# A Perceiver-style block with routed experts on one core: rests of 33 to 96 tokens as three groups, branches ahead of the last tile, context tails on 128 rows

## The chip, the cores and the metric

The kernel runs on one core of one Trainium2 chip. The metric is the device time of one execution in microseconds, the median of three runs. The names of the engines are those of the profile: PE multiplies matrices (PEld is its weight load), DVE and ACT do elementwise work, POOL issues the indirect transfers, SP issues the loads. A word on PE's records: a float32 matmul of this kernel shows as two records, a transpose as one.

## The reference, cut to what matters

All values are float32; there are 8 sequences of 64 tokens, 512 tokens of width 512.

```python
# 1. cross-attention to a context of 1601 rows per sequence
p = layernorm(x)                                   # 8 x 64 x 512
q = ctx @ W.T + b
x = x + relu(softmax(p @ q.T) @ ctx @ W.T + b)
# 2. causal linear attention with 16 heads of 64, then a gelu MLP of width 2048
h = layernorm(x)
h = h + attention(ln(h)) @ wo
h = h + gelu(ln(h) @ w1 + b1) @ w2 + b2
x = x + h
# 3. experts: 8 experts of width 1024, each token goes to its best two
m = layernorm(x); logits = m @ w_router
for e in range(8):
    out += gating[:, e] * ((silu(m @ w0[e]) * (m @ w1[e])) @ wo[e])
x = x + out
```

The number of tokens that each expert receives is data. For the inputs given, the reference's router sends 133, 104, 217, 159, 87, 132, 70 and 122 tokens to experts 0 to 7 (worked out by evaluating the reference up to its router).

## The kernel before, in words

The order of the instructions on every engine is the order in which the program writes them; no scheduler moves them.

**Cross-attention.** Tokens are taken in four tiles `t` of two sequences. `key_group(t, g)` multiplies the tile with one of four pieces of the transposed context (`ctxT`), `softmax(t)` and `turn_scores(t)` make the transposed weights `eT`, and `weigh(t, g)` multiplies them with the context rows (`ctx`), three pieces of 512 rows and then a tail. 1601 = 3 x 512 + 65, so the tail is 65 rows: it is loaded to 65 partitions (`tail`, L188), its weights are turned by one transpose (L464), and it closes the sum with two matmuls over 65 rows (L487). DVE then scales the sum by the reciprocal of the row sums (`av_sb`, L495). The context comes in through SP's queue into a ring of 12 buffers, in an order written out by hand. At the end of tile `t = 1`, `late_loads` (L408 to L412) puts five small transfers on the same queue: zeros to the spare rows of the output, zeros to a table, a bias, and `proj` twice; `centre_router` (L548) is four small matmuls.

**Experts.** The router's ranks are written to a table in DRAM; from it POOL gathers each expert's first 128 tokens (key `(e, 0)`) and the next few, 32 of them (key `(e, 1)`). `whole_tile` takes 128 tokens through one expert: four quarters `up` (L1200), silu and product, transposes `ht`, `down` (L1208); `between(k)` slips the transposes `xgt` of later tokens in between. `add_rows` scales the result on ACT (`y_sb`, L1180) and POOL adds it to the output with an indirect transfer (L1181). After each tile stands a branch, `tc.If(few_of[e] > 0)` (L1429): where the expert has 129 to 160 tokens, `group` takes the rest, up to 32 tokens, through the same weights, the four quarters side by side in four column strips of PE's array (L1238, L1249), and sums the strips with one more matmul, `fold` (L1259). Experts with more than 160 tokens are listed, and each further set of 128 tokens becomes a "big" tile behind the last expert: `all_big` (L1433) nests seven branches, and each `big_tile` loads the six weight buffers of its expert again. For these inputs the groups behind experts 0, 3 and 5 run (5, 31 and 4 tokens) and one big tile runs, the remaining 89 tokens of expert 2.

A branch that is not taken ends in a small block of its own, in which each engine waits until its own work is done, and then raises its counters by what the skipped block would have raised them.

Of the kernel before, what the change touches and what calls it, by code (L numbers as in the profile page):

```python
# [26 lines left out]
NG = LK // GK  # L27
TAIL = LK - NG * GK
SW = -(-LK // 4)
# [5 lines left out]
FQ = FE // NQ  # L35
R = P // NQ
NI = B * S // P
COLS = 4 * KC + FF // P + KC * NE
# [8 lines left out]
def perceiver_kernel(  # L47
# [127 lines left out]
    def issue_to(n):  # L175

        while issued[0] < min(n, len(order)):
            key, src = order[issued[0]]
            if in_ring(key) and len(held) >= RING:
                if held[0] not in freed:  # L180
                    return
                held.pop(0)
            if key in places_of:
                t_ = places_of[key]
                nc.sync.dma_start(t_, src)
            elif key[0] == "tail":
                t_ = tails.tile([P, 2, D], F32, tag="tail", name="_".join(str(k) for k in key))
                nc.sync.dma_start(t_[:TAIL, :, :], src)  # L188
            else:
                width = WIDTHS[key[2]] if key[0] == "ctxT" else 512  # L190
                t_ = ring.tile([P, 4, width], F32, tag="ring", name="_".join(str(k) for k in key))
                nc.sync.dma_start(t_, src)
                held.append(key)
            streamed[key] = t_
            issued[0] += 1
# [254 lines left out]
    def turn_scores(t):  # L450
# [5 lines left out]
        for g in range(NG + 1):  # L456
            bank = mm_bank(f"et_{t}_{g}")
            if g < NG:
                for j in range(4):
                    k = g * GK + j * P  # L460
                    nc.tensor.transpose(bank[:, j * P : (j + 1) * P], scores[:, k : k + P], ident)
                nc.scalar.copy(e_t[:, 4 * g : 4 * g + 4, :].rearrange("p j q -> p (j q)"), bank)
            else:
                nc.tensor.transpose(bank[:TAIL, :P], scores[:, NG * GK : LK], ident)  # L464
                nc.scalar.copy(e_t[:TAIL, 4 * NG, :], bank[:TAIL, :P])

    all_av, all_xo = {}, {}

    def weigh(t, g):
# [15 lines left out]
        if g == NG - 1:  # L485
            for h in range(2):
                nc.tensor.matmul(  # L487
                    av[h * S : (h + 1) * S, :],
                    e_t[:TAIL, 4 * NG, h * S : (h + 1) * S],
                    need("tail", t)[:TAIL, h, :],  # L490
                    start=False,
                    stop=True,
                )
            av_sb = all_av[t] = xa2.tile([P, D], F32, tag="tmp", name=f"av_sb_{t}")
            nc.vector.tensor_scalar(av_sb, av, all_rinv[t], None, ALU.mult)  # L495

# [65 lines left out]
    for t in range(NT):  # L562
# [14 lines left out]
        weigh(t, 2)  # L577
        if t == NT - 3:
            late_loads()
            centre_router()  # L580
# [530 lines left out]
    if True:  # L1111
# [36 lines left out]
        def turn_tile(key, n=P):  # L1148
# [4 lines left out]
            for c in range(KC):  # L1153
                nc.tensor.transpose(  # L1154
                    bank[:, c * n : (c + 1) * n], xg[:n, c * P : (c + 1) * P], ident[:n, :n]
                )
            xg_t = moe2.tile([P, KC, n], F32, tag=f"xgT{n}", name=f"xgT_{key[0]}_{key[1]}")
            evacuate(xg_t.rearrange("p c q -> p (c q)"), bank[:, : KC * n])
# [71 lines left out]
        def group(e, up_of, down_of):  # L1230
# [3 lines left out]
            xg_t = turned[e, 1]  # L1234
            bank = side_bank(1, f"up_{nm}")
            for c in range(KC):
                for q in range(NQ):
                    nc.tensor.matmul(  # L1238
                        bank[q * R : (q + 1) * R, :],
                        xg_t[c],  # L1240
                        up_of[q][:, c, :],
                        start=(c == 0),
                        stop=(c == KC - 1),
                    )
            h_t = hidden_t(1, gated(1, bank, nm), nm)
            bank = side_bank(1, f"yq_{nm}")
            for j in range(2):
                for q in range(NQ):
                    nc.tensor.matmul(  # L1249
                        bank[q * R : (q + 1) * R, :],  # L1250
                        h_t[:, j, q * R : (q + 1) * R],
                        down_of[q // 2][:, 2 * (q % 2) + j, :],
                        start=(j == 0),
                        stop=(j == 1),
                    )
            parts = moe2.tile([P, D], F32, tag="parts", bufs=1, name=f"parts_{nm}")
            evacuate(parts, bank)
            y = y_bank(1, f"y_{nm}")
            nc.tensor.matmul(y[:R, :], fold, parts, start=True, stop=True)  # L1259
            add_rows((e, 1), y, R, 1)  # L1260

        if True:
# [7 lines left out]


            few = moe.tile([P, NE], F32, name="few")
            more = moe.tile([P, NE, NI - 1], F32, name="more")
            nc.vector.tensor_scalar(more[:, :, 0], count, float(P + R), None, ALU.is_gt)
            nc.vector.scalar_tensor_tensor(few, count, float(P), more[:, :, 0], ALU.is_gt, ALU.subtract)
            few_i = moe.tile([1, NE], mybir.dt.int32, name="few_i")
# [3 lines left out]
            def load_few():  # L1280
                _, values = nc.values_load_multi_w_load_instructions(
                    few_i, min_val=0, max_val=1, skip_runtime_bounds_check_because=counted
                )
# [3 lines left out]
            flat = "p e i -> p (e i)"  # L1287
            control = moe.tile([1, 1 + 2 * NBIG], mybir.dt.int32, name="control")

            def list_big(k):  # L1290

                if k == 0:
# [10 lines left out]
                    listed["sums"] = sums  # L1303
                    nc.vector.tensor_copy(control[:, 0:1], sums[0:1, nmore - 1 :])
                else:
                    by_big = [P, NBIG, nmore]
# [11 lines left out]
                    for v, values in enumerate([number, which_e]):  # L1318
# [6 lines left out]
                        )  # L1325
                    nc.vector.tensor_copy(control[:, 1:], numbers[0:1, :])
                    listed["big_e"] = numbers[:, NBIG:]

            def load_big():
# [11 lines left out]
                _, experts = nc.values_load_multi_w_load_instructions(  # L1341
                    control[:, 1 + NBIG :],
                    engines=sp,
# [3 lines left out]
                )  # L1347
                return big, spots, experts

# [11 lines left out]
            def gate_big(j):  # L1361
# [11 lines left out]
                slots["big", j] += (gate,)  # L1373

            def big_tile(j):

                key = ("big", j)
                tiles = {}
                e = bass.ds(listed["experts"][j], 1)
                for q in range(NQ):  # L1380
                    tiles["up", q] = ring.tile([P, 4, 512], F32, tag="ring", name=f"big_up_{j}_{q}")
                    nc.sync.dma_start(tiles["up", q], e_up[e, q].rearrange("o p c n -> p (o c) n"))
                    if q % 2:
                        n = q // 2
                        tiles["wo", n] = ring.tile([P, 4, 512], F32, tag="ring", name=f"big_wo_{j}_{n}")
                        nc.sync.dma_start(
                            tiles["wo", n],
                            e_wo[e, n].rearrange("o p c n -> p (o c) n"),
                        )

# [8 lines left out]
                )  # L1399

            turned[0, 0] = [xg_t0[c // 2][:, c % 2, :] for c in range(KC)]
            for e in range(NE):

                def between(k, e=e):
                    if e == 0 and k == 0:
                        late_places()
                        for key in [(1, 0), (0, 1), (0, 0), (1, 1), (2, 0), (2, 1)]:
                            fetch(key, R if key[1] else P)
                    if k == (2 if e == 0 else 1) and e + 1 < NE:
                        turn_tile((e + 1, 0))  # L1410
                    if k == 2:
                        turn_tile((e, 1), R)
                    if e == 1 and k < 2:
                        list_big(k)

                up_of = [need("e_up", e, q) for q in range(NQ)]
                down_of = [need("e_wo", e, n) for n in range(2)]
                whole_tile((e, 0), up_of, down_of, between)
                if e == 0:
                    few_of = load_few()  # L1420
                if 3 <= e + 2 < NE:
                    for i in range(2):
                        fetch((e + 2, i), R if i else P)
                if e == 3:
                    listed["big"], listed["spots"], listed["experts"] = load_big()
                    listed["pairs"] = read_big(0)
                if e == NE - 3:
                    fetch_big(0, listed["pairs"])
                with tc.If(few_of[e] > 0):  # L1429
                    group(e, up_of, down_of)  # L1430

            def all_big(j):
                with tc.If(listed["big"] > j):  # L1433
                    big_tile(j)
                    if j + 1 < NBIG:
                        all_big(j + 1)

            all_big(0)


# [90 lines left out]
```

## Time and profile before

| | us |
|---|---|
| median of 3 runs (663.93 to 664.02) | 663.94 |
| the profiled execution's own time | 665.04 |
| its span, first to last instruction | 663.3 |
| PE busy | 624.8 (94%) |
| DVE, ACT, POOL busy | 175.4, 128.9, 61.8 |
| mean granted PE clock | 0.987 |

How to read it: the span begins with the cross-attention (to about 185 us), then linear attention (to about 290 us), the MLP (to about 410 us) and the router; the first expert's tile starts at 417.26 us and the last result is written behind 652.98 us. PE is busy nearly everywhere, so time comes from the places where it isn't, from the work that it is given, and from the end.

### The profile page before, as it was taken

The numbers are of one execution on the slowest core, as the hardware profiler recorded it, in microseconds if no ns is written. First come the engines' busy times: TensorE is split into PE (matmuls) and PEld (weight loads), VectorE is DVE, ScalarE is ACT, GpSimd is POOL, SyncE is SP. The second block draws the span as 40 slices with busy tenths as digits, with TensorE's granted clock in tenths as the row PEclk, the third lists the DMA queues.
The fourth block names the chain that finished last, engine by engine and source line by source line (L and its number), as shares of the span: only waits on it lengthen the run. The fifth ranks groups of instructions, "written<-read, shape, count | busy, mean of one in ns | idle before, by whom it ended". The sixth has DMA issues, their size and how long they took to land. (4 is left out here: it accounts for less than half of the span.)

```text
span 663.3 us, 6862 instructions
## 1 busy us (share of the span) xinstructions
PE 624.8 (94%) x2688; PEld 292.5 (44%) x2688; DVE 175.4 (26%) x421; ACT 128.9 (19%) x242; POOL 61.8 (9%) x82
## 2 busy tenths in 40 slices
PE   4998999899999999999999999999999899999993
PEld 3743434243444444455444458434444344344441
DVE  4011323123315878760000045311211011100100
ACT  2241222220132222031101211211111111111110
POOL 2000000000000000050000012240201202200000
PEclk9998999899999999999999999999999999999997
DMA  8999999999430303030311313139379567594611
GB/s 325 418 424 398 423 393 422 381 394 417 178 126 3 126 1 127 1 126 1 126 64 63 116 74 133 64 96 365 139 280 377 178 279 246 202 385 155 263 16 19
DMA packets 24224, 138.08 MB, mean 208 GB/s; under 512 B 4164, under 2 KB 4164, under 8 KB 11896
## 3 DMA queue, kind: packets, MB, share of 16 engines
q1 hardware_dynamic: 20056, 129.90, 49.8%
q0 software_dynamic: 3024, 6.58, 4.4%
q10 hardware_dynamic: 1104, 1.07, 0.5%
q8 instruction: 25, 0.41, 0.3%
q14 instruction: 15, 0.12, 0.0%
HBM read 132.56 MB, written 4.97 MB: 207 GB/s over the span
## 5 line engine op out<-in xcount | busy, mean ns | idle before, releaser
L1200 PE MATMUL up<-e_up,xgT 128*128 128x512 f32 x224 | 100.2, 595 | 1.2 <-PEq L1429 1.2
L1200 PEld LDWEIGHTS up<-e_up,xgT 128*128 128x128 f32 x224 | 40.9, 190 | 50.4 <-issue 50.4
L1208 PE MATMUL y<-e_wo,hidT 128*128 128x512 f32 x128 | 61.0, 599 | 0.0
L477 PE MATMUL av<-ctx,eT 128*64 128x512 f32 x192 | 51.3, 648 | 6.3 <-DMA ctx<-in_ctx_dram 6.3
L1165 DVE TENSOR_TENSOR mid<-up,act 128x256 f32<-128x256 f32 x35 | 14.8, 425 | 159.4 <-ACT act L1163 159.4
L809 PE MATMUL hid<-v_sb,w 128*128 128x512 f32 (+2 forms) x144 | 56.6, 545 | 0.0
L830 PE MATMUL mlp<-w,hid_sb 128*128 128x512 f32 x112 | 51.0, 597 | 0.0
L428 PE MATMUL sc<-ctxT,pw_t 128*64 128x401 f32 (+1 forms) x256 | 46.6, 501 | 0.0
L809 PEld LDWEIGHTS hid<-v_sb,w 128*128 128x128 f32 x144 | 26.2, 190 | 29.1 <-issue 27.3
L1163 ACT ACTIVATE act<-up 128x256 f32<-128x256 f32 x35 | 13.3, 384 | 103.7 <-PE up L1200 94.9
L1181 POOL DMA_INDIRECT out_dram<-y_sb,dst_late x11 | 16.8, 1530 | 159.9 <-ACTq L1429 103.7
L824 POOL TENSOR_TENSOR xin<-xin,b_bc 128x512 f32<-128x512 f32 x4 | 5.1, 1265 | 283.2 <-DVE rstd_h L766 279.0
L830 PEld LDWEIGHTS mlp<-w,hid_sb 128*128 128x128 f32 x112 | 20.7, 190 | 23.5 <-issue 23.4
L1208 PEld LDWEIGHTS y<-e_wo,hidT 128*128 128x128 f32 x128 | 22.4, 190 | 19.5 <-issue 19.1
L428 PEld LDWEIGHTS sc<-ctxT,pw_t 128*64 128x64 f32 x256 | 20.6, 136 | 23.4 <-issue 21.7
L477 PEld LDWEIGHTS av<-ctx,eT 128*64 128x64 f32 x192 | 14.7, 146 | 36.1 <-issue 27.5
L728 PE MATMUL wo<-wo,a_t 128*128 128x512 f32 x64 | 29.1, 600 | 0.6 <-DVE a_t L704 0.6
L617 PE MATMUL wk<-h_t,wk 128*128 128x512 f32 x64 | 29.5, 603 | 0.0
L617 PE MATMUL wq<-h_t,wq 128*128 128x512 f32 x64 | 29.4, 602 | 0.0
L537 PE MATMUL v<-wv,h_t 128*128 128x512 f32 x64 | 28.7, 597 | 0.6 <-DVE h_t L524 0.6
L702 DVE RECIPROCAL rden<-rden 128x512 f32<-128x512 f32 x8 | 26.8, 3353 | 0.3
L878 DVE TENSOR_TENSOR xs<-mlp,xs 128x512 f32<-128x512 f32 x3 | 2.1, 692 | 86.6 <-PE mlp L830 86.6
(245 smaller groups left out, 642.6 us busy)
## 6 DMA issues: line engine op xcount, KB each, us to landing
e_up<-in_L_ffn_up_dram SPq DMA_DIRECT2D x32, 1024.0 KB, 7.7
ctx<-in_ctx_dram SPq DMA_DIRECT2D x24, 1024.0 KB, 17.1
ctxT<-in_ctx_T_dram SPq DMA_DIRECT2D x24, 802.0 KB, 15.7
e_wo<-in_L_ffn_wo_dram SPq DMA_DIRECT2D x16, 1024.0 KB, 10.6
w<-in_L_attn_w_dram SPq DMA_DIRECT2D x8, 1024.0 KB, 9.8
ctxT<-in_ctx_T_dram SPq DMA_DIRECT2D x8, 796.0 KB, 16.4
big_up<-in_L_ffn_up_dram SPq DMA_DIRECT2D x4, 1024.0 KB, 7.7
wv<-in_L_attn_wv_dram SPq DMA_DIRECT2D x2, 1024.0 KB, 13.0
```

Source lines behind the costliest of these rows:

```text
L428: nc.tensor.matmul(sc[h * S : (h + 1) * S, :width], pw_t[:, c, (2 * t + h) * S : (2 * t + h + 1) * S], keys[h][:, c, :], start=(c == 0), s ...
L477: nc.tensor.matmul(av[h * S : (h + 1) * S, :], e_t[:, 4 * g + j, h * S : (h + 1) * S], rows[h][:, j, :], start=(g == 0 and j == 0), stop=F ...
L537: nc.tensor.matmul(bank, h_t[:, c, t * P : (t + 1) * P], wv_n[:, c, :], start=(c == 0), stop=(c == KC - 1))
L617: nc.tensor.matmul(bank, w[:, c, (j % 4) * P : (j % 4 + 1) * P], h_t[:, c, :], start=(c == 0), stop=(c == KC - 1),)
L702: nc.vector.reciprocal(rden, rden)
L728: nc.tensor.matmul(wo_banks[t], a_t[:, j, t * P : (t + 1) * P], wo_r[j // 4][:, j % 4, :], start=(j == 0), stop=(j == nj - 1),)
L809: nc.tensor.matmul(hid_banks[f][:, tokens], w[:, c, (f % 4) * P : (f % 4 + 1) * P], h2_t[:, c, tokens], start=(c == 0), stop=(c == KC - 1),)
L830: nc.tensor.matmul(acc[t], hid[:, t * P : (t + 1) * P], need("w2", f // 4)[:, f % 4, :], start=(f == 0), stop=(f == FF // P - 1),)
L1165: nc.vector.tensor_tensor(hid, bank[:, FQ:], act, ALU.mult)
L1181: nc.gpsimd.indirect_dma_start(out=out, out_offset=bass.IndirectOffsetOnAxis(ap=dst[:n, :], axis=0), in_=y_sb[:n, :], in_offset=None, boun ...
L1200: nc.tensor.matmul(bank, xg_t[c], up_of[q][:, c, :], start=(c == 0), stop=(c == KC - 1))
L1208: nc.tensor.matmul(y, h_t[:, j, :], w[:, 2 * (q % 2) + j, :], start=(q + j == 0), stop=(q + j == NQ))
```

## The change

Four things are altered.

1. The tail is one row shorter, 64 rows. The two sequences' tails are stacked on 128 partitions (the host lays them out so), and beside them stands the last context row, copied to 64 partitions for each sequence. The tail's weights are turned by two 64x64 matmuls against the identity; the tail's two products use two quarters of the array; the last row is added on DVE by a multiply and add, ahead of the scaling. The tail's transfer grows from 65 to 128 rows of 4 KB.
2. `late_loads` and `centre_router` stand at the end of tile 2 instead of tile 1.
3. A rest of 33 to 96 tokens is no longer a big tile: `three_groups` takes it behind the expert's own tile, as three groups of 32. The gathers of `(e, 1)` fetch 96 rows. Each expert therefore has two branches, one for three groups and one for a group. `group` itself is written in two halves of 128 hidden columns, so that silu and product of the first half run beside the second half's matmuls, and the second product is cut into halves of 256 columns.
4. The branches of experts 6 and 7 and the big tiles stand ahead of the last expert's tile, inside one more branch on "any of them". In the middle of each tile a prefetch hint names the branch ahead as likely taken. One more control value is loaded into registers on every engine after expert 3's tile. Big tiles reuse weight buffers instead of taking new ones.

The diff, cut to its core:

```diff
-TAIL = LK - NG * GK
+TAIL = LK - NG * GK - 1
+REST = 3 * R
...
-                nc.sync.dma_start(t_[:TAIL, :, :], src)
+                nc.sync.dma_start(t_, src)
...
-                nc.tensor.transpose(bank[:TAIL, :P], scores[:, NG * GK : LK], ident)
-                nc.scalar.copy(e_t[:TAIL, 4 * NG, :], bank[:TAIL, :P])
+                for h in range(2):
+                    part = slice(h * S, (h + 1) * S)
+                    nc.tensor.matmul(
+                        bank[part, :S],
+                        scores[part, NG * GK : NG * GK + TAIL],
+                        ident[part, part],
+                        start=True,
+                        stop=True,
+                    )
+                nc.scalar.copy(e_t[:, 4 * NG, :S], bank[:, :S])
...
-                    e_t[:TAIL, 4 * NG, h * S : (h + 1) * S],
-                    need("tail", t)[:TAIL, h, :],
+                    e_t[h * S : (h + 1) * S, 4 * NG, :S],
+                    need("tail", t)[h * S : (h + 1) * S, 0, :],
...
-            nc.vector.tensor_scalar(av_sb, av, all_rinv[t], None, ALU.mult)
+            nc.vector.scalar_tensor_tensor(
+                av_sb, need("tail", t)[:, 1, :], all_scores[t][:, LK - 1 : LK], av, ALU.mult, ALU.add
+            )
+            nc.vector.tensor_scalar(av_sb, av_sb, all_rinv[t], None, ALU.mult)
...
-        if t == NT - 3:
+        if t == NT - 2:
             late_loads()
             centre_router()
...
         def group(e, up_of, down_of):
...
+            for h in range(2):
+                bank = side_bank(1, f"up_{nm}_{h}")
+                for c in range(KC):
+                    for q in range(NQ):
+                        nc.tensor.matmul(
+                            bank[q * R : (q + 1) * R, : 2 * P].rearrange(split, w=2),
+                            xg_t[c],
+                            up_of[q][:, c, :].rearrange(split, w=2)[:, :, halves[h]],
+                            start=(c == 0),
+                            stop=(c == KC - 1),
+                        )
+                act = moe2.tile([P, P], F32, tag="act1", name=f"act_{nm}_{h}")
+                nc.scalar.activation(act, bank[:, :P], AF.Silu)
+                hid.append(moe2.tile([P, P], F32, tag="mid1", name=f"mid_{nm}_{h}"))
+                nc.vector.tensor_tensor(hid[h], bank[:, P : 2 * P], act, ALU.mult)
...
+            turn(0)
+            down(0, 0)
+            turn(1)
+            down(0, 1)
+            parts = []
+            for n in range(2):
+                down(1, n)
+                parts.append(moe2.tile([P, D // 2], F32, tag="parts", name=f"parts_{nm}_{n}"))
+                (nc.scalar.copy if n else nc.vector.tensor_copy)(parts[n], sums[n][:, : D // 2])
+            y = side_bank(1, f"y_{nm}")
+            for n in range(2):
+                nc.tensor.matmul(
+                    y[:R, n * D // 2 : (n + 1) * D // 2], fold, parts[n], start=True, stop=True
+                )
             add_rows((e, 1), y, R, 1)
+
+        def three_groups(e, up_of, down_of):
+            xg = fetched[e, 1]
+            bank = y_bank(1, f"xgt3_{nm}")
+            for c in range(KC):
+                nc.tensor.transpose(
+                    bank[:, c * REST : (c + 1) * REST], xg[:REST, c * P : (c + 1) * P], ident[:REST, :REST]
+                )
...
+            up(0)
+            up(1)
+            turn(0)
+            up(2)
+            turn(1)
+            down(0)
+            down(1)
+            turn(2)
+            y = side_bank(1, f"y3_{nm}")
+            folded(0)
+            down(2)
+            folded(1)
+            folded(2)
+            add_rows((e, 1), y, REST, 1)
...
-            nc.vector.tensor_scalar(more[:, :, 0], count, float(P + R), None, ALU.is_gt)
+            nc.vector.tensor_scalar(more[:, :, 0], count, float(P + REST), None, ALU.is_gt)
...
+            def few_tokens(e, up_of, down_of):
+                with tc.If(few_of[e] == 1, label=f"three_{e}"):
+                    three_groups(e, up_of, down_of)
+                with tc.If(few_of[e] == 2):
+                    group(e, up_of, down_of)
+
+            def hint_ahead(e):
+                with tc.block():
+                    tc.mark_branch_hint_location("last_branches" if e == NE - 2 else f"three_{e}", "LikelyTaken", engines=every)
...
                 def between(k, e=e):
+                    if k == 0 and e < NE - 1:
+                        hint_ahead(e)
...
-                            fetch(key, R if key[1] else P)
+                            fetch(key, REST if key[1] else P)
...
+                if e == NE - 1:
+                    with tc.If(listed["any"] > 0, label="last_branches"):
+                        few_tokens(e - 1, *last_weights)
+                        few_tokens(e, up_of, down_of)
+                        all_big(0)
...
                 whole_tile((e, 0), up_of, down_of, between)
...
-                with tc.If(few_of[e] > 0):
-                    group(e, up_of, down_of)
...
-            all_big(0)
+                if e < NE - 2:
+                    few_tokens(e, up_of, down_of)
```

`up(g)`, `turn(g)`, `down(g)` and `folded(g)` of `three_groups` are the old group's steps, of the old group's shapes, for 32 tokens each; its first group takes the tokens that `between` has already turned, the others take those of the four 96-row transposes.

## The prediction

> **What bounds the kernel now.** I read the page first, then PE's waits, four-microsecond windows over the cross-attention, and PE's timeline around the experts.
>
> ```profile
> PE 624.8 (94%) x2688; PEld 292.5 (44%) x2688; DVE 175.4 (26%) x421; ACT 128.9 (19%) x242; POOL 61.8 (9%) x82
> ```
>
> PE bounds the whole. 94% leaves 38.5 us, so a gain is either PE work taken away or one of the few places where PE stands still. The first is the context's stream:
>
> ```profile
> PE av L477 <- DMA ctx<-in_ctx_dram: 6.3, 4, 2.7
> ...
> 60.00:64.00 4.00, 3.01 (x10) 0.97 (x12) 0.65 (x1) 1.72 (x2) 0.00 (x0) 0.75 1.02 396
> 124.00:128.00 4.00, 1.31 (x4) 0.46 (x6) 1.82 (x1) 3.18 (x4) 0.00 (x0) 0.86 1.03 270
> 128.00:132.00 4.00, 4.00 (x10) 0.97 (x10) 0.00 (x0) 0.00 (x0) 0.00 (x0) 0.50 1.02 419
> ...
> 124.03 1.04 PE L477 MATMUL av<-ctx,eT 128*64 128x512 f32 x2 [0.51 <-DMA ctx<-in_ctx_dram]
> 127.73 6.16 PE L477 MATMUL av<-ctx,eT 128*64 128x512 f32 x13 [2.66 <-DMA ctx<-in_ctx_dram]
> 135.11 3.70 PE L537 MATMUL v<-wv,h_t 128*128 128x512 f32 x8
> ```
>
> Four waits of PE for context rows cost 6.3 us; the longest ends at 127.73, at the end of tile 2. The windows (busy time of the five engines, granted clock, DMA share, GB/s) show a second price: the DMA engines are full (1.02), and after a wait the clock falls to 0.50, so that the 13 matmuls take 6.16 us. From 126.9 to 133.7 it is halved, two stretches of 3.4 us. PE's next work, the values at 135.11, could have stood near 128 without wait and half clock. Later work is bound by PE again.
>
> In the experts, three things stand out: the group behind a tile, the big tile at the end, and the branches.
>
> ```profile
> 571.71 0.43 PE L1154 MATMUL xgt<-ident,xg 32*128 32x32 f32 x4
> 572.07 1.98 PE L1208 MATMUL y<-e_wo,hidT 128*128 128x512 f32 x4
> 573.99 3.64 PE L1238 MATMUL up<-e_up,xgT 128*32 128x512 f32 x32
> 578.62 0.44 PE L1171 MATMUL ht<-ident,mid 128*128 128x128 f32 x2 [0.99 <-DVE mid L1165]
> 579.66 1.92 PE L1249 MATMUL yq<-e_wo,hidT 128*32 128x512 f32 x16 [0.61 <-DVE hidT L304]
> 582.28 1.05 PE L1259 MATMUL y<-parts,fold 128*32 128x512 f32 x2 [0.69 <-ACT parts L306]
> 583.26 7.13 PE L1200 MATMUL up<-e_up,xgT 128*128 128x512 f32 x16
> ...
> 473.37 1.95 PE L1200 MATMUL up<-e_up,xgT 128*128 128x512 f32 x4 [0.30 <-PEq L1429]
> ...
> 628.90 0.65 PE L1154 MATMUL xgt_big<-ident,xg_big 128*128 128x128 f32 x4 [0.32 <-PEq L1429]
> 648.38 3.60 PE L1208 MATMUL y_big<-big_wo,hidT_big 128*128 128x512 f32 x8
> ```
>
> A group takes 9.27 us (573.99 to 583.26), 2.29 of it three stalls. The big tile occupies PE from the end of the last expert's tile (about 628.5) to about 651.9, 23.4 us. A branch not taken costs PE 0.30 us.
>
> **The change, part by part.** The profiled execution took 665.04 us, its span 663.3; the median of the runs is 663.94, 1.1 below. I make the sum against 665.04 and subtract 1.1.
>
> *Context tails and late loads.* SP's queue now carries this ahead of the late context piece:
>
> ```profile
> 104.88 0.34 SPq L408 DMA_DIRECT2D out_dram<-v_sb  x1
> 116.12 2.23 SPq L192 DMA_DIRECT2D ctx<-in_ctx_dram  x2
> ```
>
> The five late transfers hold 576 KB (256 + 32 + 256 + 2 x 16), at the 420 GB/s of these windows 1.4 us, and all go behind that piece. Each tail grows by 63 x 4 KB = 252 KB, 0.6 us, and two stand ahead of the piece. Yet the windows with a 65-row tail move less (396, 270 GB/s against 420), 1.0 to 1.5 us lost at each; if 128 rows spread over all 16 engines, that comes back and a tail is worth -0.4 to -0.6. So the piece lands 2.4 us sooner (0.2 if the dips stay): 125.3. `centre_router`, 1.0 us of PE, no longer lies ahead of the wait but behind it, so it is exposed, and PE reaches the wait earlier and idles about 2.8 us again. By the trace one such idle (2.14 us in tile 0) halves the clock for one stretch (0.75 in the window from 60), and the 3.2 us of tile 2 for two. [...] The row decides; I take one stretch, 1.7 us lost. The values then start at 125.3 + 3.7 (13 matmul records of 0.218 and the tail's 0.87) + 1.7 + 1.0 = 131.7, **-3.4** (by the rule -5.1). Range -5.5 to +0.5, the upper end being dips that stay and two stretches. The new multiply and add on DVE (0.69 us, row of the same shape at L514) and the scaling from SBUF instead of PSUM (0.55 for 0.75) add 0.5 ahead of `turn_av`; a key group or the values, 2.9 to 3.4 us of PE, lies between and hides it. Without that cover it is +0.5 at each of four tiles. On SP the late loads pass that piece and all that is queued for tiles 2 and 3 before them; they are needed at 195 us and later, so they cost nothing there; nor do the tail's two 64x64 matmuls for one transpose (0.1).
>
> *Groups (three).* PE's own slots are 3.44 + 0.22 + 1.72 + 0.86 = 6.2 (each traced duration less its 0.2 us of pipeline fill), and about 0.1 at each of four changes of array shape (the `y` after the 32-row `xgt` takes 1.92 us to its successor, not 1.72). In halves, the first half's silu and product lie under the second's matmuls, and one copy of the weights lies under the other's product; a first copy (0.6) and the last copy of the parts (0.5) remain: 7.8 against 9.27. But a group now stands behind the skipped branch for three groups, and in the built program its first matmul waits until ACT and DVE have counted that block. ACT has the tile's last scaling before it:
>
> ```profile
> 473.11 0.69 ACT L1180 ACTIVATE y_sb<-y,xg 128x512 f32<-128x512 f32 x1 [1.65 <-PE y L1208]
> 474.07 1.54 POOL L1181 DMA_INDIRECT out_dram<-y_sb,dst_late  x1 [21.30 <-ACTq L1429]
> ```
>
> The tile's last matmul ends at 473.1, ACT is free at 473.80: 1.0 us that PE waits. Net -0.47 each, **-1.4** (range -3 to +1).
>
> *Skipped branches.* Experts 1 and 4 skip two instead of one: the second finds PE idle, +0.25 each, **+0.5**. The branch ahead of the last tile replaces the one behind expert 6 (0.37), and the last tile's first matmul waits for ACT's count like a group, 1.0: **+0.6**. Each skip now jumps over 323 and 208 instructions of PE instead of 105 (rival A).
>
> *The 89 tokens of expert 2.* Three groups cost four transposes 0.44, 3 x 3.44 for `up`, 3 x 0.22, 3 x 1.72, 3 x 0.86: 19.2, interleaved so that the elementwise steps of one lie under the matmuls of another, and eight changes of shape at 0.1: 20.0. The big tile's 23.4 go: **-3.4** (range -4.4 to -2.4). Its 6 MB of weights go too, off PE's path. If that cover fails, each of the three turns shows up to 0.6, 1.8 in all, and leaves -1.6.
>
> *The end.* Now POOL passes the skipped big tiles' counts after the last transfer (the DMA share falls to 0.03 by 657.0, the span ends at 663.3); after the change no branch stands there: **-0.3** (0 to -1.5). The tail of scaling 0.69, indirect add 1.55 and landing stays.
>
> *Gathers of 96 rows* for 32: POOL's 0.94 to 0.98 us become about 1.0 each, in a queue that runs ahead; only the first, just before the first tile's turn, may be late: **+0.3** (0 to 1.5). The three more DVE operations for the flags (0.17 each) fall into 3.1 us of idle DVE from 421.7. Loads of control values and hints are done by PE's queue, which runs some 3 us ahead of the array: 0, and 0.7 in all if that lead is gone.
>
> Sum: -3.4 - 1.4 + 0.5 + 0.6 - 3.4 - 0.3 + 0.3 = -7.1. Profiled execution 657.9, median **656.8**.
>
> **The rivals.**
>
> *A: code loading (slower).*
>
> ```profile
> q8 instruction: 25, 0.41, 0.3%
> ```
>
> The kernel's instructions come through a queue in 25 fetches of 16 KB, 0.3% of 663.3 us x 16 / 25 = 1.3 us each. [...] Against it: today's skips of 105 show 0.30 us and no fetch, PE's queue reads its branch about 3 us ahead, and the hints name these branches. [...] I follow the row, as the lead would hide 1.3.
>
> *B: the context gives nothing.* Doubled tails eat what the late loads free, and dips stay: 656.8 + 3.4 = 660.2. For it: the DMA engines are full in every window; against: 1.4 us leave the queue ahead of the piece in any case.
>
> *C: all cover holds.* No half clock (-1.7), and no wait for ACT before the three groups and the last tile (4 x -0.6): about 652.7. [...] Against it: the built program's waits.
>
> **How the numbers follow.** My sum 0.60, A in full 0.13, partly exposed skips that end near no change 0.05, B 0.12, C 0.10. The likeliest gives 656.8; its own unknowns reach 654 to 659. The range takes in B and C: 652.5 to 661.5, and leaves out A. About 0.2% (1.3 us) is what a measurement can tell: faster 0.80, same 0.05, slower 0.15.
>
> **What would show it.** Right: the values (L537) start near 131.7 instead of 135.1, with one window at half clock; a group takes 7.8 us from its first matmul and starts 1.0 after the tile; three groups take 20 us; no big tile; the last indirect add starts near 646. Wrong: gaps over 1 us on PE at the branches and more fetches than 25 (A); a wait before L477's last matmuls that still ends at 127 or two stretches at half clock (B); gaps before the groups of 0.3 only (C).

## The result, and the profile after

The changed kernel takes 655.10 us (median of 5 runs, 654.75 to 655.35), the kernel before, run beside it, 663.94 (661.87 to 664.82): a ratio of 0.987, 95% interval 0.986 to 0.989. The profiled execution takes 655.10 us with a span of 653.4. It lies on its median, where that of before lay 1.1 us above: the profiles differ by 9.9 us, the medians by 8.8.

The page of the changed kernel, first the busy times, then the queue that brings code:

```profile
PE 621.1 (95%) x2950; PEld 292.5 (45%) x2950; DVE 179.3 (27%) x436; ACT 129.5 (20%) x247; POOL 62.1 (10%) x82
...
q8 instruction: 33, 0.54, 0.3%
```

PE's busy time fell only by 3.7 us, and part of that is matmuls that no longer run at half clock (the 192 records of the context product take 46.6 us instead of 51.3); more came from places where PE stood still. (A second queue of the kind that brings code, q14, shows 18 packets where it showed 15.) The cross-attention, by PE's waits, the three windows and PE's timeline:

```profile
PE av L487 <- DMA ctx<-in_ctx_dram: 1.6, 3, 1.0
...
60.00:64.00 4.00, 3.88 (x16) 1.24 (x18) 0.79 (x1) 1.72 (x2) 0.00 (x0) 1.00 1.01 420
124.00:128.00 4.00, 4.00 (x19) 1.18 (x15) 0.73 (x2) 1.74 (x3) 0.00 (x0) 1.00 1.02 430
128.00:132.00 4.00, 4.00 (x15) 2.19 (x16) 1.17 (x3) 0.00 (x0) 0.00 (x0) 1.00 1.02 430
...
123.13 3.65 PE L487 MATMUL av<-ctx,eT 128*64 128x512 f32 x14 [0.23 <-DMA ctx<-in_ctx_dram]
126.71 1.08 PE L497 MATMUL av<-tail,eT 64*64 64x512 f32 x4
127.72 1.06 PE L562 MATMUL router_sums<-col,ones 128*128 128x8 f32 x8
128.63 3.68 PE L551 MATMUL v<-wv,h_t 128*128 128x512 f32 x8
```

The stream no longer dips (430 GB/s where it was 270), the last context piece is there at 123.13 instead of 127.73, PE waits 0.23 us for it instead of 2.66, and the clock is not halved in any window from 40 us to the last matmul. The small router matmuls are exposed for 0.9 us (127.72 to 128.63), and the values still start at 128.63 instead of 135.11.

The experts on PE's timeline:

```profile
411.06 7.10 PE L1221 MATMUL up<-e_up,xgT_first 128*128 128x512 f32 x16 [0.51 <-issue]
436.04 3.66 PE L1265 MATMUL up<-e_up,xgT 128*32 128x256 f32 x64 [1.12 <-ACTq L1537]
440.79 0.64 PE L1290 MATMUL yq<-e_wo,hidT 128*32 128x256 f32 x8 [0.83 <-DVE hidT L1282]
444.22 7.13 PE L1221 MATMUL up<-e_up,xgT 128*128 128x512 f32 x16
468.43 7.11 PE L1221 MATMUL up<-e_up,xgT 128*128 128x512 f32 x16 [1.47 <-PEq L1539]
490.98 0.49 PE L1320 MATMUL xgt<-ident,xg 96*128 96x96 f32 x4
511.55 7.11 PE L1221 MATMUL up<-e_up,xgT 128*128 128x512 f32 x16 [0.30 <-PEq L1539]
567.10 7.10 PE L1221 MATMUL up<-e_up,xgT 128*128 128x512 f32 x16 [0.91 <-ACTq L1537]
623.24 7.11 PE L1221 MATMUL up<-e_up,xgT 128*128 128x512 f32 x16 [1.43 <-DVEq L1578]
641.36 3.60 PE L1229 MATMUL y<-e_wo,hidT 128*128 128x512 f32 x8
```

A group takes 8.18 us (436.04 to 444.22), but waits 1.12 us before it starts; the three groups run from 490.98 to about 511.2; two skips in a row cost 1.47 us behind expert 1 and 0.91 behind expert 4; the last tile waits 1.43. The last matmul ends at 644.96 and the span at 653.4, 8.4 us later; before, it was 651.98 and 663.3, 11.3 us. The end shows in the windows, first of before, then of after (busy times, clock, DMA share, GB/s):

```profile
654.00:657.00 3.00, 0.00 (x0) 0.00 (x0) 0.00 (x0) 0.00 (x0) 0.53 (x1) 0.82 0.64 86
657.00:659.00 2.00, 0.00 (x0) 0.00 (x0) 0.00 (x0) 0.00 (x0) 0.00 (x0) 0.50 0.02 2
659.00:663.30 4.30, 0.00 (x0) 0.00 (x0) 0.00 (x0) 0.00 (x0) 0.00 (x0) 0.50 0.00 0
```

```profile
649.00:651.00 2.00, 0.00 (x0) 0.00 (x0) 0.00 (x0) 0.00 (x0) 0.00 (x0) 0.59 0.48 83
651.00:653.40 2.40, 0.00 (x0) 0.00 (x0) 0.00 (x0) 0.00 (x0) 0.00 (x0) 0.50 0.00 0
```

Almost nothing moves for 6.3 us at the end of before, for 2.4 at the end of after. The trace's records of POOL's queue say why: before, POOL first waits for the last transfer (to 657.67), then raises the count of the skipped big tile (657.80, 1.0 us), and starts its last drain (the record DRAIN at the kernel's end) at 659.00, 3.5 us. After, it starts that drain at 645.73, beside the transfer, and it ends at 652.53.

The sum of the prediction against the two profiles:

| part | predicted | measured | read from |
|---|---|---|---|
| up to the first expert's tile | -3.4 | -6.2 | 417.26 to 411.06 |
| three groups with the waits before them | -1.4 | -0.1 | groups -1.09, -1.10, -1.10; from a tile's start to its group +1.19, +1.07, +0.89 |
| second skip of experts 1 and 4 | +0.5 | +1.8 | +1.16, +0.62 from tile to tile |
| branches ahead of the last tile | +0.6 | +0.8 | expert 6's tile to expert 7's +1.39, expert 7's own tile -0.56 |
| the 89 tokens | -3.4 | -3.3 | 23.40 of the big tile; expert 2's stretch grows by 20.11 |
| the end | -0.3 | -2.9 | 11.32 to 8.44 |
| gathers of 96 rows | +0.3 | (0.1) | the first group starts 1.19 later behind its tile, 1.12 of it the wait in front; counted in the second row, not again in the sum |
| sum | -7.1 | -9.9 | profiled executions |

### The profile page after: what moved, and what is told of

Read it like the earlier page. It is cut to its first block, busy times and chain, and to the rows that moved or that the text cites. A ratio compares the mean times of both kernels' runs of the same rounds, so it can differ in the third digit from the quotient of the medians.

```text
span 653.4 us, 7473 instructions
## 1 busy us (share of the span) xinstructions
PE 621.1 (95%) x2950; PEld 292.5 (45%) x2950; DVE 179.3 (27%) x436; ACT 129.5 (20%) x247; POOL 62.1 (10%) x82
## 3 DMA queue, kind: packets, MB, share of 16 engines
q10 hardware_dynamic: 1104, 1.07, 0.5%
## 5 line engine op out<-in xcount | busy, mean ns | idle before, releaser
L487 PE MATMUL av<-ctx,eT 128*64 128x512 f32 x192 | 46.6, 597 | 1.6 <-DMA ctx<-in_ctx_dram 1.6
L1202 POOL DMA_INDIRECT out_dram<-y_sb,dst_late x12 | 18.3, 1524 | 181.0 <-ACT y_sb L1201 60.1
L844 PEld LDWEIGHTS mlp<-w,hid_sb 128*128 128x128 f32 x112 | 20.7, 190 | 23.5 <-issue 23.4
```

The source lines that it names most:

```text
L487: nc.tensor.matmul(av[h * S : (h + 1) * S, :], e_t[:, 4 * g + j, h * S : (h + 1) * S], rows[h][:, j, :], start=(g == 0 and j == 0), stop=F ...
L844: nc.tensor.matmul(acc[t], hid[:, t * P : (t + 1) * P], need("w2", f // 4)[:, f % 4, :], start=(f == 0), stop=(f == FF // P - 1),)
L1202: nc.gpsimd.indirect_dma_start(out=out, out_offset=bass.IndirectOffsetOnAxis(ap=dst[:n, :], axis=0), in_=y_sb[:n, :], in_offset=None, boun ...
```

## The experiments

Each time is a median beside runs of the kernel before, which took 663.9, 663.9, 664.1 and 664.7 us in the four sets.

### The cross-attention, part by part

**Late loads alone.** The kernel before with one edit:

```diff
-        if t == NT - 3:
+        if t == NT - 2:
             late_loads()
             centre_router()
```

> The kernel before, with only the late loads and the small router matmuls moved from the end of tile 1 to the end of tile 2. If the late transfers were what held the context piece up (rival), nearly all of the 6.2 us that the changed kernel is ahead at the first expert's tile appears: the values start near 129, some -5 to -6 us. If the 65-row tails cost more than I summed (theory), only the 1.4 us of the 576 KB and perhaps one stretch of half clock appear: the wait for the context still ends near 126, the values start at 132 to 133, some -2 to -3 us.

It took 661.91 us, ratio 0.997 (0.996 to 0.998). Its windows, then PE's timeline:

```profile
60.00:64.00 4.00, 2.70 (x10) 0.97 (x12) 0.70 (x1) 1.72 (x2) 0.00 (x0) 0.82 0.99 366
124.00:128.00 4.00, 2.18 (x10) 0.63 (x10) 1.82 (x1) 3.40 (x4) 0.00 (x0) 1.00 0.96 268
...
61.30 4.92 PE L477 MATMUL av<-ctx,eT 128*64 128x512 f32 x13 [2.40 <-DMA ctx<-in_ctx_dram]
126.40 3.22 PE L477 MATMUL av<-ctx,eT 128*64 128x512 f32 x13 [1.82 <-DMA ctx<-in_ctx_dram]
131.75 3.68 PE L537 MATMUL v<-wv,h_t 128*128 128x512 f32 x8
```

The piece lands 1.33 us sooner (1.4 were summed), the dips stay (268 GB/s), and the values start at 131.75, a little sooner than the theory's 132 to 133, because the clock stays full here. The rival, that the late loads were the whole, is out.

**Tails alone.** The kernel before with the edits of the tails (lines `TAIL` to `av_sb` of the diff) and nothing else.

> The kernel before, with only the tails of 128 rows. Theory: the 65-row transfers lower the rate of the whole stream (270 to 396 GB/s in their windows against 424), so the larger transfer is the quicker one: no window under 415 GB/s up to 125 us, the context piece lands 2 to 3 us sooner, the values start at 129 to 132, some -3 to -5 us. Rival: the tails cost their bytes, 252 KB or 0.6 us each, and the values start at 135 to 136.5, 0 to +1.2 us.

659.95 us, ratio 0.994 (0.992 to 0.996); a window and PE's timeline:

```profile
124.00:128.00 4.00, 3.30 (x14) 1.05 (x14) 0.53 (x1) 1.72 (x2) 0.00 (x0) 1.00 1.02 431
...
124.70 3.65 PE L485 MATMUL av<-ctx,eT 128*64 128x512 f32 x14 [1.30 <-DMA ctx<-in_ctx_dram]
```

With a transfer that is twice as large the stream is quicker: the dips are gone, and the piece lands at 124.70, 3.0 us sooner. The first expert's tile starts at 411.74, 5.5 us earlier than before. So the tails are the larger of the two. Why 65 rows cost so much is not shown. The DMA engines were not idle in the dip (a share of 1.03 at 270 GB/s, of 1.02 at 431): by the trace's DMA records the 8 KB packets of the context itself took 487 ns on average there, 309 ns in the same window with 128 rows.

**Both parts.** The two edits together, the experts as before.

> The kernel before with both parts of the cross-attention (tails of 128 rows, late loads and router behind tile 2), the experts as before. Theory: the cross-attention's share of the gain is 6.2 us and independent of the experts: the first expert's tile starts at 411.1 and the whole is 6.0 to 6.4 shorter. Rival: part of it is given back in the experts, because their weights land no sooner; then the experts show waits for weights and the whole is under 5 us shorter.

659.45 us, ratio 0.993 (0.991 to 0.996). In the profile the first expert's tile starts at 411.12 and the span is 657.4, 5.9 shorter; against the median it is 4.5, since the profile of before lay 1.1 above its median and this one 0.2 below. The experts give nothing back (the first group starts 23.8 us behind its tile, as before). The parts overlap: -3.4 and -5.5 make -6.1 to the first expert's tile. The landings do add up (1.3 and 3.0 sooner alone, 4.5 together, 127.73 to 123.19); what is counted twice is the half clock in front of the values, some 2.9 us, which either part alone takes away (the 13 matmuls take 3.22 us with the late loads alone, where they took 6.16).

### The group in halves

The changed kernel with the function `group` as it was before.

> The changed kernel with the former group for up to 32 tokens (not in halves). Theory: the halves save the stalls inside a group, 9.27 to 8.17 us, and the gap before a group stays at 0.8 to 1.1: three groups of 9.27, +3.3 us against the changed kernel, about 658.4. Rival: the halves start a group no better because the wait in front of it moves; then the gap falls to 0.3 and the whole is +1 us or less.

658.36 us, 3.3 more than the changed kernel. The groups take 9.31, 9.32 and 9.32 us, the gaps before them are 1.13, 1.02 and 0.82. The halves are worth 1.1 us a group, and what eats them is the wait in front.

### Where the branches stand

**One branch around both.**

```diff
-                with tc.If(few_of[e] == 1, label=f"three_{e}"):
-                    three_groups(e, up_of, down_of)
-                with tc.If(few_of[e] == 2):
-                    group(e, up_of, down_of)
+                with tc.If(few_of[e] > 0, label=f"three_{e}"):
+                    with tc.If(few_of[e] == 1):
+                        three_groups(e, up_of, down_of)
+                    with tc.If(few_of[e] == 2):
+                        group(e, up_of, down_of)
```

> The changed kernel with both branches of an expert inside one branch on 'any rest', so that an expert without a rest skips once. Theory: the gaps of 1.47 us behind expert 1 and 0.91 behind expert 4 come from the second skip, whose branch PE can read only after the first skip has waited for PE itself (467.16, 0.96 us); with one skip they are 0.3 to 0.4, -1.6 us, about 653.5; the gaps before the three groups stay at 0.8 to 1.1. Rival: the price is the fetch of code behind the blocks (rival A), and jumping over both at once costs it as well: gaps of about 1 us stay and the time is within 0.5 us of 655.1.

661.57 us, 6.5 slower than the changed kernel: both forecasts missed. 0.97 us of it, in the profile, lies ahead of the first expert's tile, which the edit doesn't touch. PE's timeline:

```profile
468.32 7.10 PE L1221 MATMUL up<-e_up,xgT 128*128 128x512 f32 x16 [0.30 <-PEq L1537]
567.65 7.10 PE L1221 MATMUL up<-e_up,xgT 128*128 128x512 f32 x16 [0.30 <-PEq L1537]
598.45 1.08 PE L1290 MATMUL yq<-e_wo,hidT 128*32 128x256 f32 x8 [3.34 <-DVE hidT L1282]
629.95 7.13 PE L1221 MATMUL up<-e_up,xgT 128*128 128x512 f32 x16 [2.67 <-ACTq L1579]
```

The two gaps that were to go did go (0.30 each, although both blocks are jumped at once). But the group of expert 5 waits 3.34 us inside, with half clock after it (1.08 us for eight matmuls that took 0.64), and the last tile 2.67. The branches stand elsewhere in the code and the hint now names another one: a first sign, no more, that fetches of code decide.

**Group, else three groups.**

```diff
+                with tc.If(few_of[e] > 0, label=f"three_{e}"):
+                    with tc.If(few_of[e] == 2) as cmp:
+                        group(e, up_of, down_of)
+                    with cmp.Else():
+                        three_groups(e, up_of, down_of)
```

> The changed kernel with one branch on 'any rest' and inside it group, else three groups. Theory: a group no longer stands behind a skipped block, so it doesn't wait for ACT's and DVE's counts: the gap before it falls from 0.8 to 1.1 to 0.1, -2.8 us over three; experts 1 and 4 skip once, -1.6; the skip behind the three groups is gone, -0.2; about 650.5. Rival: the padding of counts moves to the end of the block, and the tile behind a group waits for ACT's last scaling instead; then the gaps are behind the groups and only the -1.6 remain, about 653.5.

651.94 us (651.08 to 653.36), ratio to before 0.982 (0.980 to 0.984): faster than both kernels. PE's timeline:

```profile
434.92 3.66 PE L1265 MATMUL up<-e_up,xgT 128*32 128x256 f32 x64
466.12 7.10 PE L1221 MATMUL up<-e_up,xgT 128*128 128x512 f32 x16 [0.30 <-PEq L1537]
537.70 0.64 PE L1290 MATMUL yq<-e_wo,hidT 128*32 128x256 f32 x8 [1.94 <-DVE hidT L1282]
592.06 0.64 PE L1290 MATMUL yq<-e_wo,hidT 128*32 128x256 f32 x8 [1.32 <-DVE hidT L1282]
```

No group waits in front, and no tile behind a group waits either. That settles the 1.0 us: it was the wait for ACT's and DVE's counts of a skipped block. The groups of experts 3 and 5 wait 1.94 and 1.32 us inside, where expert 0's waits 0.80: together 1.7 us more, which is about the 1.4 us missing to the forecast.

### The hints

**None.** The changed kernel without the call of `hint_ahead`.

> The changed kernel without the hints in the middle of each tile. If the hints hide the fetches (rival A in the form that it takes without them), each skip that today shows 0.3 to 1.5 us shows about 1 us more: +4 to +9 us. Theory: PE reads the first branch 3 us ahead of the array and the fetch takes about 1 us, so the hints do nothing for the first skip of a pair and don't name the second: within 0.5 us of 655.1; the fetches of code stay at 33, give or take 2.

663.87 us (661.6 to 666.9), ratio to before 1.000 (0.998 to 1.001): without the hints the whole change brings nothing. PE's timeline:

```profile
570.45 8.72 PE L1221 MATMUL up<-e_up,xgT 128*128 128x512 f32 x16 [3.25 <-issue]
602.85 1.08 PE L1290 MATMUL yq<-e_wo,hidT 128*32 128x256 f32 x8 [3.33 <-DVE hidT L1282]
```

My theory is wrong here: the loss has the size that rival A allowed (+4 to +9), but not its form of about 1 us more at each skip. The gaps behind experts 1 and 2 stay at 1.46 and 0.30 us. Behind expert 4, PE's first branch takes from 563.73 to 567.22 by the records of its queue, 3.49 us, where it took 0.34 with the hint, and a fetch starts inside it, at 564.64; PE stands 3.25 us and then runs at half clock. The other loss is inside the groups of experts 3 and 5 (1.82 and 3.33 us for 0.83). The profile puts those waits down to DVE, but DVE waits for ACT, and ACT for PE: in expert 5's group PE's count is raised at 601.84, although the records of `up`, whose ends are modelled, end at 599.27. So that time is lost on PE itself; by what is not shown. There are 35 fetches for 33: when they come counts for more than their number.

**None, with group or three groups in one branch.**

> The form with one branch on 'any rest' and group or three groups inside it, without the hints. If what the hints save is a matter of where code lies and not of the pairs of branches, it loses as much as the changed kernel lost without them: +5 to +9 us on 651.9, with single gaps of 1 to 3.3 us behind the branches. If it was the second skip of a pair that needed them, the loss is under 2 us.

668.72 us (664.8 to 673.1), ratio 1.007 (1.004 to 1.010), 16.8 more than with hints, more than I allowed for. One line of its timeline says where: the jump from a group's end over the three groups' code.

```profile
446.92 9.64 PE L1221 MATMUL up<-e_up,xgT 128*128 128x512 f32 x16 [3.82 <-issue]
```

The tiles behind the groups of experts 3 and 5 wait 4.09 and 4.22 us in the same way. In the records of PE's queue six branches take 3.3 to 4.7 us, where the same six take 0.3 to 0.9 with the hints. So it does not take the pair of branches; that the place of the code decides is my reading of it.

**Later, and earlier.** The hint ahead of the tile's last product instead of in its middle; then, in another kernel, at the tile's start.

> The same form with the hint some 10 us later in each tile, ahead of its last two products. If the hinted code is pushed out again by the fetch of the tile's own next code, the later hint is the better one: the waits of 1.94 and 1.32 us inside the groups of experts 3 and 5 fall to 0.80 and the time to about 650.5. If the hint needs the time in front of the branch (a fetch takes about 1 us, and two may be needed), it is equal or worse: 651.5 to 655.

> The form with group or three groups inside one branch, the hint at the start of each tile instead of in its middle (some 12 us earlier). If the hint only needs time in front of the branch, it is as good as in the middle, 651 to 653. If the code that it brings is pushed out again by the tile's own code, it is as bad as none, about 668. The late hint (some 10 us later than the middle, 659.0) says that time is needed; this run says whether there is also a too early.

Late: 658.95 us (656.2 to 665.3), ratio 0.994 (0.991 to 0.998). Early: 652.44 (651.6 to 653.3), ratio 0.982 (0.980 to 0.985), the same as in the middle. A hint can come too late (the tiles behind the groups of experts 0 and 3 wait 3.77 and 4.89 us), not too early here: given 23 us ahead of the tile's branch it works as well. The two kernels have the same instructions in another order, so it is the hint's moment and not the place of later code that differs. Time alone doesn't explain it: the late hint in expert 0's tile (429.6) is still 12.8 us ahead of the jump that stalls (442.4), and a fetch takes 0.88 to 1.41 us in the records of the changed kernel. What a hint does in that time, no run shows.

### The end

The changed kernel with the branches of experts 6 and 7 behind their own tiles, and the big tiles last.

> The changed kernel with the branches of experts 6 and 7 and of the big tiles behind their tiles, as before the change. Theory: the end is where the branch costs: POOL has to wait for the last transfer and raise counts of 0.6 to 1.0 us each, and only then starts its last drain of 3.5 us, which now runs beside the transfer; +3 us or more from the last matmul to the end (8.4 becomes 11.4 to 13), against 1.43 us saved before the last tile and 0.9 to 1.5 lost for the pair behind expert 6: +2.5 to +5 us. Rival (my sum): the end is worth 0.3 us and the kernel is 0 to 1 us faster than the changed one.

664.16 us (661.1 to 665.7), ratio 1.000 (0.999 to 1.002), 9.1 more than the changed kernel. In the profile the last matmul ends at 648.69 and the span at 660.4, 11.7 us: the end costs 3.3 us more, as the theory had it, and POOL's queue shows it again (count raised 655.02 to 656.02, drain to 659.55). The rest is not the end: expert 5's group waits 2.79 us inside and runs at half clock, and five more fetches of code stand in the trace.

### A big tile for the 89 tokens

```diff
-            nc.vector.tensor_scalar(more[:, :, 0], count, float(P + REST), None, ALU.is_gt)
+            nc.vector.tensor_scalar(more[:, :, 0], count, float(P + R), None, ALU.is_gt)
```

> The changed kernel with the former bound of 32 on a rest, so that the 89 tokens of expert 2 are a big tile again, now ahead of the last tile and in expert 6's weight buffers. Theory of the sum: three groups cost 20.1 us against 23.4 of a big tile, +3.3 us; and since the six weight loads (6 MB) now wait for expert 6's own use of the buffers, PE waits some 8 to 12 us for them: 664 to 671 in all. Rival: the tile on its own costs no more than the three groups and the loads are hidden; 655 to 657.

680.80 us, ratio 1.024 (1.021 to 1.027), 25.7 more than the changed kernel.

```profile
612.51 0.94 SPq L1518 DMA_DIRECT2D e_up<-in_L_ffn_up_dram  x2
623.49 1.08 PE L1168 MATMUL xgt_big<-ident,xg_big 128*128 128x128 f32 x4 [13.96 <-PEq L1539]
625.25 9.80 PE L1221 MATMUL up_big<-e_up,xgT_big 128*128 128x512 f32 x16 [0.68 <-ACT xgT_big L307]
```

Both forecasts missed (664 to 671, 655 to 657). PE stands 13.96 us, but not for weights. By the records of its queue it spends that time in the four skipped branches of experts 6 and 7, which now stand in a row with no hint of their own: 3.29, 2.65, 4.78 and 5.32 us from 605.96 to 622.89, with a fetch of code inside each. The six loads, issued from 612.51 to 616.15, are there when PE gets to them; no wait for one follows. So this run is no test of 20.1 against 23.4 us, nor does it show what reusing the buffers costs. It shows a price that the changed kernel escapes only while its branch on "any of them" is not taken.

## Why the prediction was right or wrong

The forecast of 656.8 is 1.7 us from the measured 655.1, which is in part luck, for steps that missed cancel: the cross-attention and the end gave 5.4 us more than summed, the experts 2.6 less; and the 1.1 us by which the profile of before lay over its median were not to be taken from that of after.

*The tails and late loads* were right in kind. The late loads' 1.4 us measured 1.33. The tails were mis-sized: summed -0.4 to -0.6 each for two, which is 1.0, measured 3.0. I counted the dips of the two tails ahead of the piece; the third window, 124 to 128, holds the deepest dip (1.5 us) and the piece was landing in it. That the 128 rows help by spreading over all 16 engines, as I supposed, no run shows.

*The clock.* I expected an idle of 2.8 us and one stretch at half clock. The idle is 0.23 us, so there is none. The -5.1 beside the -3.4 came nearer to the measured -6.2, but it takes an idle of 2.8 us ahead of the late piece to cost no clock, and no run shows that: the idle there was 0.23 us, with the late loads alone 1.82. The length of one idle stretch does not tell the two cases apart: 2.14 us in the kernel before and 2.40 with the late loads alone were followed by half clock, 1.00 (tile 1 of the kernel before) and 1.82 (late loads alone) were not, and 2.67 us in front of the last tile (one branch around both) was not either. A fixed grid of windows fits: in each trace the clock changes only at whole multiples of 3.41 us from its other changes (in the kernel before at 62.00, 65.41, 126.85, 133.68 and 655.92). Windows of that grid, the first three from the kernel before, then late loads alone, then one branch around both (PE's busy time first, then the other engines', then the clock):

```profile
123.44:126.85 3.41, 1.12 (x4) 0.19 (x2) 1.82 (x1) 2.66 (x3) 0.00 (x0) 1.00 1.04 290
126.85:130.26 3.41, 2.53 (x6) 0.77 (x8) 0.00 (x0) 0.94 (x2) 0.00 (x0) 0.50 0.99 364
130.26:133.68 3.42, 3.42 (x10) 0.95 (x8) 0.00 (x0) 0.00 (x0) 0.00 (x0) 0.50 1.01 429
124.01:127.42 3.41, 1.59 (x8) 0.45 (x8) 1.82 (x1) 2.81 (x3) 0.00 (x0) 1.00 0.99 257
628.20:631.61 3.41, 1.66 (x4) 0.87 (x5) 0.00 (x0) 0.00 (x0) 1.56 (x1) 1.00 0.39 46
```

PE is busy for 1.12 us of the first, and the next is halved; it is busy for 1.59 and 1.66 us of the last two, and the clock stays full behind them. Over all fourteen traces, from the first record of the clock on (at 14.21 us in the kernel before), every full-clock window in which PE was busy for up to 0.448 of the time is followed by a halved one (15 of them ahead of the kernel's end), and none with 0.454 or more is. A halved window with PE busy for up to 0.80 is followed by another halved one, and full clock comes back only behind one that is busy throughout, as in tile 2 of the kernel before, which lost two (busy for 2.53 us of the first, 3.42 of the second). The bound is read from modelled matmul ends and is no finer than that.

*Groups.* The gap of 1.0 measured 0.82 to 1.12, and group-or-else removed it. The group itself takes 8.18 us instead of 7.8: the copy of the first weights waits 0.83 instead of 0.6, and the rest of the difference is spread. Net -0.1 instead of -1.4.

*Second skips.* 0.25 each was wrong: 1.16 and 0.62. The first skip makes PE wait for its own work, so PE reads the second branch with no lead left, and that branch takes 0.96 us behind expert 1 (467.16 to 468.12) and 0.41 behind expert 4 in its queue's records. No fetch starts inside either, so this is not rival A in small; why one takes longer than the other stays open.

*Rival A.* I put it aside because the skips of before showed 0.30 us and PE's queue ran 3 us ahead. The number held; the reason held only in part. A in full meant a wait for code at each of the nine skips (experts 0, 2, 3, 5 and the last tile once, 1 and 4 twice); no run shows that. Without the hints the kernel loses 8.8 us, at a few places: 3.25 us behind expert 4, and 1.82 and 3.33 us inside the groups of experts 3 and 5. PE's lead did hide part of one branch: ahead of the last tile the branch takes 3.72 us without the hint, and the tile waits 1.26. In all fourteen traces 24 of PE's branches take 2.0 to 5.4 us, and 23 of them have a fetch of code inside; of the 207 that take up to 1.0 us, one has. The price is not the 1.3 us of one fetch that I took: in all but one of the 23 the branch ends 1.2 to 1.5 us behind its fetch's end, and the fetch starts 0.3 to 3.0 us behind the branch's start (in the kernel before, the branch at 649.07 takes 3.64 us, its fetch runs from 650.09 to 651.31).

*Last tile and the 89 tokens* came out as summed (+0.8 for +0.6, -3.3 for -3.4); 20.1 for 20.0 us of three groups rests on the two traces alone, since the run that was to test it did not.

*The end* failed by 2.6 us. I read the 6 us without work as fixed and took only POOL's counting as removable. Its last drain started behind that counting, at 659.00; without the branch it starts at 645.73, beside the transfer. With the branch put back the end cost 3.3 us more.

*Rival B* is refuted by the tails alone. *C* came true in its first half, full clock; the waits for ACT went only with another form of the branch.

## What to carry to other kernels

A transfer of another shape than the rest can slow a whole full stream (270 GB/s in the window with a tail of 65 rows, 431 with 128); weigh it by the rate of the windows around it, not by its bytes. A skipped branch cost what the next instruction waited for: counts of other engines (0.82 to 1.12 us in front of the groups), the own queue's lead (0.96 us on PE's queue for the second branch behind expert 1), and fetches of code (3.82 to 4.22 us behind the groups without hints); look at all three, write alternatives as if and else inside one branch (651.94 us for 655.10), and give the hint well ahead (651.94 us in the middle of the tile, 658.95 ahead of its last product). Let no branch stand between the last transfer and the end (3.3 us here).

## What the runs showed of the hardware that was not expected

- Of the 24 branches that take 2.0 to 5.4 us on PE's queue, 23 have a fetch of code inside; a fetch alone takes 0.88 to 1.41 us in the trace of the changed kernel. PE stood up to 4.22 us for one such branch without a hint, and 13.96 us for four in a row. What makes the fetch start up to 3.0 us late stays open.
- In these traces the clock changed only on a fixed grid of 3.41 us: a window with PE busy for up to 0.448 of it was followed by a halved one, a window with 0.454 or more was not, and full clock came back only behind a halved window that was busy throughout.
- Kernels whose branches lack a timely hint also scatter: 661.6 to 666.9 and 664.8 to 673.1 without hints, 656.2 to 665.3 with late ones, against 654.8 to 655.4 for the changed kernel.
- The tails alone narrowed the scatter as well (659.8 to 660.2, beside 661.7 to 665.2 for the kernel before in the same set). The half clock coming and going is the likely cause: in that set the three runs of the kernel before under 662.2 us had a granted clock of 0.993 or 0.994, the four above 664.8 one of 0.986 or 0.987.
